# One gather of nine edge blocks as single-row fetches on SyncE, with SyncE's order written out

## The chip, the cores and the metric

The kernel runs on one core of a Trainium2 chip. The metric is device time in microseconds (us) of one execution; lower is better. A core has engines with their own instruction streams: TensorE (PE, matrix products), VectorE (DVE), ScalarE (ACT), GpSimd (POOL) and SyncE (SP). They meet through semaphores. DMA transfers are issued from the queues of SyncE, ScalarE and GpSimd and run on 16 shared DMA engines.

## What is computed

A graph layer over 8192 nodes of 256 channels and 131072 edges, sorted by destination. The part that the change touches is the message passing; the rest is attention inside groups of 32 nodes, dense layers and a layer norm:

```python
ea  = edge_attr @ w_e + b_e                       # [131072, 64] @ [64, 256]
msg = relu(x[src] + ea)                           # x[src]: a gather of rows of x
agg = segment_sum(msg, dst, num_segments=8192)
t = x + agg
h_local = bn(relu(t @ w1 + b1) @ w2 + b2 + x)
h_attn  = bn(attention(x in groups of 32, 4 heads) @ out_w.T + out_b + x)
out = h_local + h_attn
out = bn(out + relu(out @ m_w1 + m_b1) @ m_w2 + m_b2)
y = layernorm(x + out)
```

## The kernel before

Edges are worked in 128 blocks of 1024 (`BE`), two blocks (a pair) per turn of the main loop; nodes in 16 chunks of 512 (`CH`), eight blocks to a chunk.

One block passes through these steps. `gather` (L151) issues eight indirect DMAs from GpSimd; each fetches 128 rows of 1 KB, the source rows of 128 edges, into the tile `xs`, which has four buffers, so four blocks. The first 20 blocks (`NX`) gather from `x`; later ones from `xb`, a copy of `x` with the bias `b_e` added, which `copy_load` and `copy_store` (L594, L599) make in the first seven pairs. `load_edges` (L166) brings the edge attributes with four DMAs from SyncE into `ea` (two buffers). `edge_transpose` (L182, VectorE) turns them, which frees the `ea` buffer; `edge_products` (L190) multiplies them by `w_e` into PSUM; `edge_messages` (L214) adds products and gathered rows on VectorE (L223), in two halves per block, which frees the `xs` buffer, and ScalarE applies the relu (L227). `edge_hot`, `edge_sums` (L239) and `edge_place` (L259) make the segment sums with one-hot matmuls and add them to the chunk's transposed nodes `xT` (L276).

The node work is four streams of generators: `attention_front` (L409: load of the node rows `xn`, transposes, q and k), `attention_back` (L437: v, scores at L461, softmax, block-diagonal weights `bd` at L488, attention output `oT` at L496, output layer at L508), and `dense` (L517: the layers at L527, the sum with `xn` into `y` at L567, layer norm, and the store of `y` at L580). The class `Work` hands them out: `run(us)` takes steps from the streams in turn until their stated prices add up to `us`, and a stream that yields `REST` is passed over in the next calls: the count of 2 falls by one at the start of each call. A chunk's `xn` is loaded when its front begins, and a REST follows (L411, L412). `xn`, `xT` and `hA` have four buffers, `y` has one.

The order of the work: PE's order is as the program states it (`manual_schedule(engines={PE})`, L670). VectorE and ScalarE follow the stated order up to block 26 (`NV`) and after that the scheduler's; SyncE's queue has the scheduler's order throughout. In the main loop (L708 to L739) a pair issues its gathers for the next pair, then products, next edges and messages of the first block, sums of the pair before, the same of the second block, and node work in three calls, `run(0.3 * per)`, `run(0.2 * per)` and `run(0.5 * per)`, with the copies, the placing and the one-hots between. From block 104 (`TAIL`) on a planner (L741 to L786) decides by the times at which it expects each block's rows (`came`, 10.06 us per block) which step comes next. SyncE has one queue: a DMA that waits for its buffer holds up all behind it.

The functions that the change touches, as they were:

Of the kernel before, what the change touches and what calls it, by code (L numbers as in the profile page):

```python
# [8 lines left out]

FP = mybir.dt.float32  # L10
I32 = mybir.dt.int32
AF = mybir.ActivationFunctionType
ALU = mybir.AluOpType
AX = mybir.AxisListType
PSUM = bass.MemoryType.PSUM
DRAM = bass.MemoryType.DRAM
PE = mybir.EngineType.PE

P = 128
N, C, E, ED, H, NPG = 8192, 256, 131072, 64, 4, 32  # L20
# [3 lines left out]
NB = E // BE  # L24
# [20 lines left out]
RS = 1.0 / (1.0 + 1e-5) ** 0.5  # L45
LN_EPS = 1e-5
REST = -1.0


def slack(b):  # L50
# [21 lines left out]
def gnn_kernel(ctx: ExitStack, tc: tile.TileContext, x, src, dst, edge_attr, w, out):  # L72
# [31 lines left out]

    srci = const.tile([P, NB, TB], I32, name="srci")
    rel = const.tile([P, NB, TB], FP, name="rel")
    wrow = const.tile([P, NB], FP, name="wrow")
    width = const.tile([1, 1], I32, name="width")
    we = const.tile([P, C], FP, name="we")
# [36 lines left out]
        return pps.tile([P, 2, CH], FP, name="pe", tag="pe", bufs=2)  # L146


    xs_of = {}

    def gather(b):  # L151
        xs = epool.tile([P, NH, TJ, C], FP, name="xs", tag="xs", bufs=4)
        for h in range(NH):
            for j in range(TJ):
                idx = srcd[:, b * NH + h, j : j + 1] if b < ND else srci[:, b, h * TJ + j : h * TJ + j + 1]
                nc.gpsimd.indirect_dma_start(  # L156
                    out=xs[:, h, j, :],
                    out_offset=None,
                    in_=x if b < NX else xb[:, :],
                    in_offset=bass.IndirectOffsetOnAxis(ap=idx, axis=0),  # L160
                )
        xs_of[b] = xs
# [42 lines left out]
                    )  # L205
            pe_of[b, h] = pe

    def next_edges(b):
        if b < NB:
            edge_transpose(b)  # L210
        if b + 2 < NB:
            load_edges(b + 2)

    def edge_messages(b):  # L214

        xs = xs_of.pop(b)
        msg = msg_of[b] = epool.tile([P, NH, TJ, C], FP, name="msg", tag="msg", bufs=3)
        n = 2 if b < NB - 1 else 1
        for h in range(0, NH, 2):
            pe = pe_of.pop((b, h))  # L220
            for u in range(0, 2, n):
                hs = slice(h + u, h + u + n)
                nc.vector.tensor_add(  # L223
                    msg[:, hs].rearrange("p u i c -> p i u c"), pe[:, :, u : u + n, :],
                    xs[:, hs].rearrange("p u i c -> p i u c"),
                )
                nc.scalar.activation(msg[:, hs], msg[:, hs], AF.Relu)  # L227

    def edge_hot(b):
# [54 lines left out]
    with tc.tile_pool(name="setup", bufs=1) as sp:  # L284
# [122 lines left out]


    def attention_front(n0, st, pool, bank):  # L409
        if "xn" not in st:  # L410
            load_nodes(n0, st, pool)  # L411
            yield REST  # L412
        xn = st["xn"]
        xT = st["xT"] = pool.tile([P, KC, CH], FP, name="xT", tag="xT", bufs=4)
        hA = st["hA"] = pool.tile([P, KC, CH], FP, name="hA", tag="hA", bufs=4)
        for k in range(KC):
            ps = bank()
            for t in range(TN):
                nc.tensor.transpose(ps[:, t * P : (t + 1) * P], xn[:, t, k * P : (k + 1) * P], ident)
            nc.scalar.copy(xT[:, k, :], ps)  # L420
            nc.scalar.activation(
                hA[:, k, :], xT[:, k, :], AF.Identity, scale=s12[:, k : k + 1], bias=cA[:, k : k + 1]
            )
        yield 0.9

        qk = st["qk"] = pool.tile([P, 2 * KC, CH], FP, name="qk", tag="qk")
        for o in range(2 * KC):
            ps = bank()
            for k in range(KC):
                nc.tensor.matmul(  # L430
                    ps, inT[:, k, o * P : (o + 1) * P], xT[:, k, :], start=(k == 0), stop=(k == KC - 1)
                )
# [81 lines left out]
            st["done"] = o == KC - 1  # L514
            yield 1.7

    def dense(n0, st, pool, bank, t_a=0, t_z=TN, own=("h1", "m1", "zT", "y", "")):  # L517

        assert st["done"]
        nt = t_z - t_a  # L520
# [50 lines left out]
        rstd = pool.tile([P, TN], FP, name="rstd", tag="rstd" + own[4])  # L571
        nc.scalar.activation(rstd[:, :nt], mv[:, :nt, 1], AF.Sqrt, bias=eps_t)
        st["dense"] = t_z == TN
        yield 0.9 * part
        nc.vector.reciprocal(rstd[:, :nt], rstd[:, :nt])
        for t in range(nt):
            nc.vector.tensor_scalar(
                y[:, t, :], y[:, t, :], mv[:, t, 0:1], rstd[:, t : t + 1], ALU.subtract, ALU.mult
            )
        nc.sync.dma_start(out[ds(n0 + t_a * P, nt * P), :].rearrange("(t p) c -> p t c", p=P), y)  # L580
        yield 0.0


# [83 lines left out]
    PER_X = 4.2  # L667
    OTHER = ("vn", "qk", "oT", "pr", "o")
    placed = -1
    with tc.manual_schedule(engines={PE}):  # L670

        def last_of(c, t_z=TN):

# [2 lines left out]
        def summed(c, t_z=TN):  # L676
            last = last_of(c, t_z)
            return lambda: placed >= last and chunk[c].get("done") and not xp_of and b > 2

        for c in range(NCH):  # L680
            st, before, same = chunk[c], chunk[c - 1], chunk[c - 4]
            front = attention_front(c * CH, st, npool, bank)
            if c < 2:
                next(front)
            work.add(
                FRONT,
# [21 lines left out]
        while b < TAIL:  # L708
# [21 lines left out]
            copy_store(b // 2 - 1)  # L730
            copy_load(b // 2)
            if sums:
# [13 lines left out]
        while l < NB:  # L746
# [21 lines left out]
            elif t >= times[2]:  # L768
                if p + 2 < NB:
                    gather(p + 2)  # L770
                edge_products(p)
                next_edges(p + 2)
                edge_hot(p)
                t += 2.1
                p += 1
# [8 lines left out]
            else:  # L784
                t = work.step(t, min(times))
        work.finish()  # L786
    fast.close()


# [121 lines left out]
```

## Time and profile before

| | us |
|---|---|
| median of 3 runs | 2020.08 (2013.88 to 2028.74) |
| the profiled execution | 2009.84 |
| its span, first to last instruction | 2008.1 |
| PE busy | 1441.2 (72%) |
| POOL busy | 980.5 (49%) |
| VectorE, ScalarE busy | 784.8 (39%), 590.0 (29%) |
| mean granted TensorE clock | 0.82 of full speed |
| 1024 gathers (L156), each | 0.946 (median) |
| additions of messages (L223), each | 1.207 (128x1024), two of 0.657 (128x512) |
| DMAs of edge attributes (L172), issue on SyncE, each | 0.432 |

In the profile's lines a name with L is a line of the kernel; "x16" counts instructions; a wait is named after what ended it, "issue" is time in which the engine waited for nothing that the profile shows, and "remote" or "another core or an unknown queue" a release whose origin the records don't show. The ends of matmuls are modelled, and matmuls are pipelined, so a recorded matmul may still be at work. The page's throttle row gives the granted TensorE clock in tenths for 40 slices of the span.

### The profile page before, as it was taken

Reading aid. Unit: us, or ns where it says so; the run is one execution under the profiler, and the core shown is the slowest. Engines: PE = TensorE matmul, PEld = TensorE weight load, DVE = VectorE, ACT = ScalarE, POOL = GpSimd, SP = SyncE. Lnnn points to the kernel's source line nnn. Section 1 sums busy time; section 2 is a strip of 40 time slices with the busy share of each in tenths; the row PEclk is TensorE's granted clock in tenths of the full one; section 3 lists DMA queues with packets and bytes.
Section 4 is the critical chain, followed back from the end, with each engine's and each line's share of the span. In section 5 each row is a group of like instructions: output and inputs, shape, how many; then the busy total and the mean of one; then the engine's idle time right before and its main releaser. Section 6 shows DMA issues by size and latency. Waiting matters only on the chain.

```text
span 2008.1 us, 20804 instructions
## 1 busy us (share of the span) xinstructions
PE 1441.2 (72%) x7635; PEld 811.8 (40%) x7635; DVE 784.8 (39%) x1349; ACT 590.0 (29%) x840; POOL 980.5 (49%) x1032
## 2 busy tenths in 40 slices
PE   2787777786686867678587776876668687777667
PEld 1444434443343434344344333443334344343445
DVE  3444524433333333333435234351433434353434
ACT  1322322332323223232323323232232322333224
POOL 7455545454454444455364453544535354554540
PEclk7887888787787868788798887878779787897879
DMA  7586534443343434344344342443424343443430
GB/s 199 172 249 203 178 101 108 128 123 108 100 114 110 110 112 105 95 129 121 97 126 126 97 124 78 121 120 90 142 68 121 99 121 103 124 113 109 130 100 12
DMA packets 148904, 240.33 MB, mean 120 GB/s; under 512 B 27934, under 2 KB 112188, under 8 KB 148028
## 3 DMA queue, kind: packets, MB, share of 16 engines
q0 software_dynamic: 49152, 134.28, 24.2%
q1 hardware_dynamic: 98556, 104.65, 18.2%
q8 instruction: 62, 1.02, 0.2%
q14 instruction: 46, 0.38, 0.1%
q10 hardware_dynamic: 1088, 0.00, 0.0%
HBM read 222.06 MB, written 16.78 MB: 119 GB/s over the span
## 4 chain that ended last, share of the span: by engine, by line
PE 41%; another core or an unknown queue 29%; DVE 11%; issue 9%; ACT 7%; DMA 2%; DVEq 0%; SPq 0%; POOL 0%; ACTq 0%
PE at L527 12%; PE pe L203 9%; PE pw L246 6%; PE at L430 4%; DVE msg L223 4%; PE at L508 3%; PE l L267 2%; ACT msg L227 2%; PE pe L198 2%; ACT pr L471 1%; PE at L444 1%; DVE bd L488 1%; DVE eaT L185 1%; PE at L564 1%
## 5 line engine op out<-in xcount | busy, mean ns | idle before, releaser
L156 POOL DMA_INDIRECT xs<-xb,srci x864 | 818.7, 948 | 843.3 <-DVE msg L223 494.0
L227 ACT ACTIVATE msg<-msg 128x1024 f32<-128x1024 f32 (+1 forms) x258 | 269.8, 1049 | 520.8 <-DVE msg L223 430.1
L223 DVE TENSOR_TENSOR msg<-pe,xs 128x1024 f32<-128x1024 f32 (+1 forms) x258 | 304.2, 1195 | 141.2 <-remote 55.3
L203 PE MATMUL pe<-we,eaT 64*128 64x256 f32 x2048 | 308.3, 432 | 35.3 <-issue 17.9
L246 PE MATMUL pw<-msg,oh 128*32 128x256 f32 x2048 | 225.1, 451 | 108.2 <-issue 96.7
L203 PEld LDWEIGHTS pe<-we,eaT 64*128 64x128 f32 x2048 | 219.2, 213 | 157.8 <-issue 101.9
L156 POOL DMA_INDIRECT xs<-in_x_dram,srci x144 | 143.7, 998 | 121.0 <-DVE msg L223 41.9
L246 PEld LDWEIGHTS pw<-msg,oh 128*32 128x32 f32 x2048 | 83.1, 122 | 235.5 <-issue 202.3
L527 PE MATMUL at<-hA,mw 128*128 128x512 f32 (+2 forms) x304 | 135.8, 580 | 38.4 <-ACT oT L503 37.2
L185 DVE STREAM_TRANSPOSE eaT<-ea 128x512 f32<-128x512 f32 x128 | 90.2, 704 | 163.3 <-PE pe L203 88.0
L430 PE MATMUL at<-xT,inT 128*128 128x512 f32 x256 | 131.9, 643 | 8.3 <-ACT qk L433 3.6
L276 DVE TENSOR_TENSOR xT<-l,xT 128x352 f32<-128x352 f32 (+14 forms) x107 | 44.0, 433 | 227.2 <-remote 167.4
L527 PE MATMUL at<-xT,w 128*128 128x512 f32 (+2 forms) x152 | 87.9, 711 | 60.1 <-DVE xT L276 33.8
L527 PE MATMUL at<-m,mw 128*128 128x512 f32 (+2 forms) x304 | 119.7, 536 | 0.9 <-issue 0.8
L267 PE MATMUL l<-oh,ws 128*128 128x160 f32 (+4 forms) x512 | 89.0, 312 | 37.6 <-ACT ws L252 29.4
L267 PEld LDWEIGHTS l<-oh,ws 128*128 128x128 f32 x512 | 78.1, 201 | 68.9 <-ACT ws L252 37.9
L471 ACT COPY pr<-pe 32x256 f32<-32x256 f32 x128 | 46.4, 362 | 191.4 <-remote 138.2
L527 PE MATMUL at<-h,w 128*128 128x512 f32 (+2 forms) x152 | 77.4, 640 | 32.7 <-ACT h L534 23.5
L508 PE MATMUL at<-oT,outT 128*128 128x512 f32 x128 | 72.5, 695 | 35.8 <-ACT oT L503 23.1
L527 PEld LDWEIGHTS at<-hA,mw 128*128 128x128 f32 x304 | 57.8, 207 | 92.8 <-issue 48.8
L543 ACT ACTIVATE m<-at,vec 128x512 f32<-128x512 f32 (+2 forms) x76 | 46.7, 618 | 121.9 <-remote 67.7
L433 ACT ACTIVATE qk<-at,vec 128x512 f32<-128x512 f32 x64 | 43.7, 685 | 129.3 <-PE at L430 58.1
(111 smaller groups left out, 1260.2 us busy)
## 6 DMA issues: line engine op xcount, KB each, us to landing
ea<-in_edge_attr_dram SPq DMA_DIRECT2D x512, 128.0 KB
xs<-xb,srci POOLq DMA_INDIRECT x864
xn<-in_x_dram SPq DMA_DIRECT2D x16, 512.0 KB
out_dram<-y SPq DMA_DIRECT2D x14, 512.0 KB
xp<-in_x_dram SPq DMA_DIRECT2D x10, 512.0 KB
xb<-xp SPq DMA_DIRECT2D x10, 512.0 KB
xp<-in_x_dram SPq DMA_DIRECT2D x3, 1024.0 KB
xb<-xp SPq DMA_DIRECT2D x3, 1024.0 KB
```

What stands on the lines that cost most here:

```text
L156: nc.gpsimd.indirect_dma_start(out=xs[:, h, j, :], out_offset=None, in_=x if b < NX else xb[:, :], in_offset=bass.IndirectOffsetOnAxis(ap= ...
L185: nc.vector.transpose(eaT, ea[:, QR:].rearrange("p (g d) -> p g d", d=ED)[:, :, :QR])
L203: nc.tensor.matmul(pe[:, i, u, :], eaT[rows, h + u], we[rows, :], start=(b >= NX), stop=True, skip_group_check=True)
L223: nc.vector.tensor_add(msg[:, hs].rearrange("p u i c -> p i u c"), pe[:, :, u : u + n, :], xs[:, hs].rearrange("p u i c -> p i u c"),)
L227: nc.scalar.activation(msg[:, hs], msg[:, hs], AF.Relu)
L246: nc.tensor.matmul(pw[h * WN : (h + 1) * WN, i, :], oh[:, h * TJ + j, :], msg[:, h, j, :], start=(j == 0), stop=(j == TJ - 1), skip_group_ ...
L267: nc.tensor.matmul(l2[:, k, at : at + wn], ws[:, i, k * P : (k + 1) * P], oh2[:, i, :wn], start=(i == 0 and k == 0), stop=(i == last), ski ...
L430: nc.tensor.matmul(ps, inT[:, k, o * P : (o + 1) * P], xT[:, k, :], start=(k == 0), stop=(k == KC - 1))
L471: nc.scalar.copy(pr[q, :, 2 * hh : 2 * hh + 2, :].rearrange("p t s k -> p s t k"), two4[q, :, :, q])
L508: nc.tensor.matmul(ps, outT[:, k, o * P : (o + 1) * P], oT[:, k, :], start=(k == 0), stop=(k == KC - 1))
L527: nc.tensor.matmul(ps, wt[:, k, o * P : (o + 1) * P], act[:, k, :], start=(k == 0), stop=(k == nk - 1))
L543: nc.scalar.activation(m1[:, o, :], layer(mw1, KC, o, hA), AF.Relu, bias=v_("m_b1", o))
```

## The change

In nine blocks (17, 31, 44, 57, 70, 83, 96, 109, 122) the last of the eight gathers is left out. Its 128 rows are fetched one by one by SyncE into a tile `xr` (two buffers): a register load takes 16 byte offsets at a time from `srcs`, a clamped and scaled copy of the source indices, and each row is a DMA of 1 KB. The main loop issues 20 rows per pair at five points, the tail 10 per block. The second half of such a block's messages is three additions in place of one.

SyncE's queue now keeps the stated order too. The loads of edges are put off by one or two points in the pair (`catch_up`, about half a pair), the store of a chunk's `y` by four points (two pairs), and the node rows of chunk c+4 are loaded two points after chunk c's sum with `xn`, ahead of the front that uses them; the front still rests. The third call of node work, `run(0.5 * per)`, is split in 0.3 and 0.2.

In the built orders GpSimd has 1015 gathers instead of 1024; SyncE has 1152 row DMAs and 72 register loads more; the matmuls are the same ones in a partly different order.

```diff
+ROW = 4 * C
+RT = NH * TJ - 1
+ROW_BLOCKS = (17, *range(31, NB, 13))
+RB, RL = 10, 16
...
+    def row_stream():
+        for b in ROW_BLOCKS:
+            while len(xr_of) > 1 or not (b < NX or copied[0]):
+                yield 0
+            xr = xr_of[b] = epool.tile([P, C], FP, name="xr", tag="xr", bufs=2)
+            for e0 in range(0, P, RL):
+                _, rows = nc.values_load_multi_w_load_instructions(
+                    srcs[b : b + 1, e0 : e0 + RL], engines=[SP], min_val=0, max_val=(N - 1) * ROW,
...
+                for i, row in enumerate(rows):
+                    p = (e0 + i) % EQ * QR + (e0 + i) // EQ
+                    nc.sync.dma_start(xr[p : p + 1, :].bitcast(U8), flat[b >= NX][ds(row, ROW)].unsqueeze(0))
+                    if e0 + i == P - 1:
+                        xr_full.add(b)
+                    yield 1
...
+    def fetch_rows(n):
+        for _ in range(n):
+            next(row_by_row, None)
...
     def gather(b):
...
+                if b in ROW_BLOCKS and h * TJ + j == RT:
+                    continue
...
+    def put_off(turns, do):
+        later.append([turns, do])
+
+    def catch_up(n=1):
+        for entry in list(later):
+            entry[0] -= n
+            if entry[0] <= 0:
+                later.remove(entry)
+                entry[1]()
+
-    def next_edges(b):
+    def next_edges(b, turns=0):
...
+            if turns:
+                put_off(turns, lambda: load_edges(b + 2))
+            else:
+                load_edges(b + 2)
...
     def edge_messages(b):
...
+                if b in ROW_BLOCKS and h + u + n == NH:
...
+                    nc.vector.tensor_add(msg[:, hs, 0, :], pe[:, 0, u : u + n, :], xs[:, hs, 0, :])
+                    for v in range(u, u + n - 1):
+                        nc.vector.tensor_add(msg[:, h + v, 1, :], pe[:, 1, v, :], xs[:, h + v, 1, :])
+                    nc.vector.tensor_add(msg[:, NH - 1, 1, :], pe[:, 1, u + n - 1, :], xr)
...
+        nc.vector.tensor_scalar(srcs, srci_r[:, RT * P : (RT + 1) * P], 0.0, float(N - 1), ALU.max, ALU.min)
+        nc.vector.tensor_scalar(srcs, srcs, float(ROW), None, ALU.mult)
...
-        if "xn" not in st:
-            load_nodes(n0, st, pool)
+        if "rested" not in st:
+            if "xn" not in st:
+                load_nodes(n0, st, pool)
             yield REST
...
+        catch_up(1000)
         y = pool.tile([P, nt, C], FP, name="y", tag=own[3])
...
+            put_off(2, load_ahead)
...
+        if turns:
+            put_off(turns, store)
+        else:
+            store()
...
-    with tc.manual_schedule(engines={PE}):
+    with tc.manual_schedule(engines={PE, SP}):
...
-                work.add(DENSE, summed(c), dense(c * CH, st, npool, bank))
+                work.add(DENSE, summed(c), dense(c * CH, st, npool, bank, turns=4))
...
-                next_edges(b + 2)
+                next_edges(b + 2, 1)
                 edge_messages(b)
+            fetch_rows(2 * RB // 5)
...
-            next_edges(b + 3)
+            next_edges(b + 3, 2 if b else 1)
             edge_messages(b + 1)
+            fetch_rows(2 * RB // 5)
             work.run(0.3 * per)
+            catch_up()
+            fetch_rows(2 * RB // 5)
...
             work.run(0.2 * per)
+            catch_up()
+            fetch_rows(2 * RB // 5)
             for i in blocks:
                 edge_hot(i)
-            work.run(0.5 * per)
+            work.run(0.3 * per)
+            fetch_rows(2 * RB // 5)
+            work.run(0.2 * per)
...
                 edge_products(p)
+                catch_up()
                 next_edges(p + 2)
+                fetch_rows(RB)
```

More of the change, by code (lines that the diff above doesn't have):

```diff
@@ L11 @@
 I32 = mybir.dt.int32
+U8 = mybir.dt.uint8
 AF = mybir.ActivationFunctionType
@@ L17 @@
 PE = mybir.EngineType.PE
+SP = mybir.EngineType.SP
+ACT = mybir.EngineType.Activation
 P = 128
@@ L106, in gnn_kernel @@
     rel = const.tile([P, NB, TB], FP, name="rel")
+    srcs = const.tile([P, P], I32, name="srcs")
     wrow = const.tile([P, NB], FP, name="wrow")
@@ L146, in bank2 @@
         return pps.tile([P, 2, CH], FP, name="pe", tag="pe", bufs=2)
-    xs_of = {}
+    xs_of, xr_of, xr_full = {}, {}, set()
+    flat = [a.bitcast(U8).rearrange("n c -> (n c)") for a in (x, xb[:, :])]
+    copied = [False]
+    def row_stream():
[6 more added lines that the diff above has]
+                    srcs[b : b + 1, e0 : e0 + RL], engines=[SP], min_val=0, max_val=(N - 1) * ROW,
+                    skip_runtime_bounds_check_because="the indices are clamped to the rows of x when they are kept",
+                )
+                for i, row in enumerate(rows):
[4 more added lines that the diff above has]
+                    yield 1
+    row_by_row = row_stream()
+    def fetch_rows(n):
+        for _ in range(n):
+            next(row_by_row, None)
     def gather(b):
@@ L206, in edge_products @@
             pe_of[b, h] = pe
-    def next_edges(b):
+    later = []
+    def put_off(turns, do):
[7 more added lines that the diff above has]
+    def next_edges(b, turns=0):
         if b < NB:
@@ L515, in attention_back, with dense @@
             yield 1.7
-    def dense(n0, st, pool, bank, t_a=0, t_z=TN, own=("h1", "m1", "zT", "y", "")):
+    def dense(n0, st, pool, bank, t_a=0, t_z=TN, own=("h1", "m1", "zT", "y", ""), turns=0):
         assert st["done"]
@@ L573, in dense, with load_ahead @@
         st["dense"] = t_z == TN
+        if turns and n0 // CH + 4 < NCH:
+            c = n0 // CH + 4
+            def load_ahead():
+                if "xn" not in chunk[c]:
+                    load_nodes(c * CH, chunk[c], pool)
+            put_off(2, load_ahead)
         yield 0.9 * part
@@ L579, in dense, with store @@
             )
-        nc.sync.dma_start(out[ds(n0 + t_a * P, nt * P), :].rearrange("(t p) c -> p t c", p=P), y)
+        def store():
+            nc.sync.dma_start(out[ds(n0 + t_a * P, nt * P), :].rearrange("(t p) c -> p t c", p=P), y)
+        if turns:
+            put_off(turns, store)
+        else:
+            store()
         yield 0.0
```

14 lines of the change are left out of this document (9 added, 5 removed).

## The prediction

> **What bounds the kernel now.** I read the page's busy table first, then the waits of GpSimd, then the chain that ended last, then the timeline of one stretch in which the chain names no engine, and last the waits of SyncE's queue.
>
> The busy table and the throttle row show no engine that is full:
>
> ```profile
> PE 1441.2 (72%) x7635; PEld 811.8 (40%) x7635; DVE 784.8 (39%) x1349; ACT 590.0 (29%) x840; POOL 980.5 (49%) x1032
> ...
> PEclk7887888787787868788798887878779787897879
> ```
>
> POOL, which issues the 1024 gathers, is busy for half of the span. One gather takes 0.946 us and 0.30 us pass before the next, so a run of them goes at 1.25 us each. The rest of POOL's time is waiting for the messages that free an `xs` buffer:
>
> ```profile
> POOL xs L156 <- DVE msg L223: 535.9, 51, 21.2
> POOL xs L156 <- issue: 292.0, 946, 2.8
> POOL xs L156 <- DVE oh L256: 141.0, 18, 16.2
> ```
>
> So POOL works in bursts: between 250 and 1650 us the trace has 45 bursts of 16 gathers (two blocks), each 19.7 us long, with a pause of 11.2 us on average behind it. 23 of the 44 pauses last 5.8 to 8.5 us, the other 21 last 11.4 to 21.2 us. That is what the kernel's time is made of in this stretch: bursts and pauses. What keeps the messages late? The chain gives a share that it can put on no engine:
>
> ```profile
> PE 41%; another core or an unknown queue 29%; DVE 11%; issue 9%; ACT 7%; DMA 2%; DVEq 0%; SPq 0%; POOL 0%; ACTq 0%
> ```
>
> The timeline of the burst at 507 us shows what this is. (Columns: start, duration, engine, line, operation; in brackets the idle time before and what ended it.)
>
> ```profile
> 507.16 0.94 POOL L156 DMA_INDIRECT xs<-xb,srci  x1 [18.97 <-DVE msg L223]
> ...
> 511.33 1.35 PE L267 MATMUL l<-oh,ws 128*128 128x160 f32 x8
> ...
> 521.44 0.69 ACT L503 ACTIVATE oT<-at,vec 128x512 f32<-128x512 f32 x1 [6.92 <-remote]
> ...
> 525.92 0.95 POOL L156 DMA_INDIRECT xs<-xb,srci  x1 [0.31 <-issue]
> ...
> 529.95 0.62 DVE L276 TENSOR_TENSOR xT<-l,xT 128x448 f32<-128x448 f32 x1 [18.59 <-remote]
> ...
> 540.06 1.23 DVE L223 TENSOR_TENSOR msg<-pe,xs 128x1024 f32<-128x1024 f32 x1 [4.84 <-PE pe L203]
> ...
> 543.28 0.95 POOL L156 DMA_INDIRECT xs<-xb,srci  x1 [16.41 <-DVE msg L223]
> ```
>
> The matmuls of L267 are recorded at 511.3, but VectorE, which waits for nothing but their result, goes on at 529.95, 3.1 us after the last gather of the burst ended (525.92 + 0.95). The records of PE run ahead of its work. PE is behind for most of the burst, catches up after it, then come the messages, and they start the next burst. In the table of windows PE is busy 5.06 of 14.37 us in 512.5 to 526.9 (share 0.35) and 12.64 of 16.41 us in 526.9 to 543.3 (share 0.77). Over the 45 bursts the late ends of PE's work lie 1.6 or 3.1 us behind the end of the burst again and again. Why PE is slow while gathers run, the trace does not say; that it is, it does.
>
> SyncE's queue is not in this:
>
> ```profile
> SPq L172 <- DVE eaT L185: 1118.8, 76, 33.2
> SPq L282 <- DVE st L569: 149.9, 8, 25.5
> SPq L580 <- DVE y L577: 136.7, 11, 42.4
> ```
>
> It waits for free `ea` buffers for more than half of the span, and the transposes of L185 waited for an edge load once, 1.4 us in all.
>
> **The change, part by part.** The sum is made on the profiled execution: 2009.84 us, its span 2008.1. That is 0.5% under the median of 2020.08, so the result is scaled by 1.0051 at the end.
>
> *Nine gathers leave POOL.* 9 x 1.25 = 11.3 us of bursts. If the next burst starts that much earlier each time, all of it is gained; if PE only needs its work done, less. In the cycles with short pauses (half of them) the pause holds little but the landing and the messages: full 1.25 us. In those with long pauses PE gets 0.35 x 1.25 = 0.44 us less done inside the burst and makes it up at 0.77: 0.57 us, leaving 0.68. The mean is 0.97, times 9: **-8.7 us**. Bounds -11.3 and 0 (a burst that is shorter without PE being done sooner).
>
> *Messages of these nine blocks.* One addition of 128x1024 (1.20 us) becomes one of 128x512 (0.66, the two of the last block) and two of 128x256 (nearest: the half-size addition of L567, 0.425): 1.51, so +0.31 x 9 = 2.8 us, on the path where the freed buffer starts the next burst. Four or five of the nine are second blocks of a pair, whose buffers the burst reaches 8 gathers later. **+1.4**; bounds 0 and 2.8.
>
> *1152 row fetches and 72 register loads on SyncE.* Price of a row, from its smallest and its costliest DMA: 0.231 (1 KB for `vec`) and 0.568 us (64 rows for `we`); a register load is 0.50 (the one of `width`). 20 rows per pair of blocks are 4.6 to 11.4 us, loads 0.6, the eight edge loads 8 x 0.43 = 3.5: 9 to 16 us per pair, and the shortest cycle has 26.1. In the tail 10 rows per block are 5.2 to 7.8 us with its edge loads, and a block there takes 15. The cover is the 1118.8 us in which SyncE waits for `ea` buffers. By the built order a block's rows are all issued well before its messages (block 31: in the pair before), so no message waits for them. **0**; where the cover goes, see the rivals. The bytes are those of the gathers they replace.
>
> *Edge loads, stores, node rows.* In the stated order SyncE still stops at each edge load until its buffer is free, so a load is late only by what is put in front of it: up to 16 rows, 3.7 to 9 us. It is needed a pair later (26 us or more). Stores two pairs later: `y` is written again four pairs later, and a forced catch-up stands before it. Node rows ahead: nobody waited for them (PE waited 0.2 us before L419, for an edge load). Queued behind a waiting node load or store are edge loads and rows; that wait (149.9 and 136.7 us) exists today and hides in the same slack. **0**; at best the 1.4 us of the one late edge load.
>
> *Two VectorE operations at the start* (128x128 on `srcs`): at most 0.41 us each by L577's 128x256. They stand before the copies of `srci`, behind which the first gathers from `x` wait, but PE transposes meanwhile. **+0.4**; bounds 0 and 0.8.
>
> *PE's order.* `work.run` is now called four times per pair, and a REST lasts two calls, so attention resumes sooner. I counted matmuls of the built orders at full-clock prices (0.43 us for 512 columns and pass) between the last score matmul and the first `oT` matmul of a chunk: mostly 11 to 20 us before, 9 to 17 after, but 1.6 in the second chunk and 5.4 in a late one (the least before was 4.5, and PE did not wait there). The softmax between them took 11.1 us in the second chunk and 14 to 32 us in later ones, where VectorE was itself held by PE. If PE waits, edge products are queued behind. High: 11.1 - 1.6 = 9.5, and 22.5 - 7.0 (5.4 at share 0.77) = 15.5, together 25. Low: 0, since a late chain is mostly late through PE; a gain is not excluded either, see below. I take **+4**, nearest to the low end, because the case with 4.5 cost nothing.
>
> Sum: -8.7 + 1.4 + 0.4 + 4 = -2.9; 2009.84 - 2.9 = 2006.9; times 1.0051: **2017 us**. Ends: -11.3 gives 2009, +28.6 gives 2049.
>
> **The rivals.** Less than 1% either way (2000 to 2040) is about what a measurement of this kernel can't tell from no change.
>
> *The shorter burst gives nothing* (same; 0.10). PE's work is unchanged, and if its lateness is its own, the burst only happens to end with it. For: PE's share 0.77 even behind the bursts. Against: the ends at 1.6 and 3.1 us behind the burst. 2017 + 8.7 = 2026 us. Beside it: the Trainium skill (SBUF — State Buffer, section on the two separate sides) says that DMA and engine accesses use separate ports and can't slow each other; by that rule this rival holds. The trace, 0.35 against 0.77, speaks for some contention, though not for which.
>
> *PE waits for the softmax* (slower; 0.22). Place: L496 behind L488. It decides when the softmax takes longer than the cover, in the two chunks above all: +25 instead of +4, and the full 2.8 for messages: 2009.84 - 8.7 + 28.6 = 2029.7, scaled 2040. A wait that pushes a message past the end of a burst also turns a short pause into a long one, 7 us into 14 for one of them: 2047 us.
>
> *SyncE becomes the bound* (slower; 0.05). It decides when a row costs more than (26.1 - 4.1)/20 = 1.1 us. At 1.5 us a pair takes 34 us where the mean cycle is 30.9: 58 pairs x 3.1 = 180, about 2190. Against: SyncE issues one DMA after the other every 0.23 to 0.57 us, while the first landing comes 2.1 us (median of 512 edge loads) after the issue, so it does not wait for each. Beside it: the Trainium skill (DMA: Bandwidth & Descriptors, rules for kernel authors and the anatomy of one DMA) gives a fixed 2 us per DMA and advises against many small ones; if the rows went one at a time, 20 x 2 + 4 = 44 us per pair, some 2700 us, an estimate by that page.
>
> *The new order shortens pauses* (faster; 0.18). 21 pauses are long because attention or dense steps stand in front of the edge products. The finer calls move these steps; if three of 21 fall from 16 to 7 us, 27 us go: 1990. The same lottery can lose as much.
>
> **How the numbers follow.** The forecast has 0.45, with the first rival 0.55 near 2017 to 2026, of which 0.02 reaches below 2000 and 0.02 above 2040. Faster 0.18 + 0.02 = 0.20; same 0.51; slower 0.22 + 0.05 + 0.02 = 0.29. The range reaches from the faster rival, 1990, to just above the softmax rival, 2050; outside are SyncE as the bound and the far parts of both, 0.2.
>
> **What would show it.** Right: 1015 gathers; nine bursts of 18.5 us; the same late PE behind bursts; SyncE still waiting hundreds of microseconds for `eaT`; no wait of VectorE for `xr`. Wrong: L496 waiting for `bd` by more than 10 us; `eaT` waiting for edge loads; rows above 1 us each; a mean pause other than 11 us by more than 1, which 45 times over is more than all else here.

## The result, and the profile after

The changed kernel takes 2074.73 us (median of 4 runs, 2063.42 to 2079.32), the kernel before 2017.86 in the same runs: ratio 1.0265, 95% interval 1.0206 to 1.0323. It is 57 us slower. The forecast was 2017, with a range from 1990 to 2050.

One thing has to be known for the numbers that follow: the kernel before took 2018 to 2019 us beside this result and in one group of the experiments, and 1324 us in the other four groups, though runs of both kinds came from a chip of the same number. So each kernel is compared only with the kernel before in its own group of runs; I write "the 2018 setting" and "the 1324 setting".

The profiled execution of the changed kernel has a span of 2072.2 us, 64.1 more than before. The busy table:

```profile
PE 1415.5 (68%) x7635; PEld 819.6 (40%) x7635; DVE 782.9 (38%) x1369; ACT 590.5 (28%) x838; POOL 969.9 (47%) x1023
...
PEclk7777787878688888878778797878888788798779
```

The engines are busy for about as long as before (TensorE 1415.5 us against 1441.2) and the granted clock is nearly the same (0.811 against 0.822); the 64 us are waiting. The waits of GpSimd:

```profile
POOL xs L191 <- DVE msg L281: 508.3, 50, 32.0
POOL xs L191 <- issue: 287.3, 933, 2.8
POOL xs L191 <- DVE oh L314: 193.0, 17, 22.9
POOL xs L191 <- DVE msg L278: 46.0, 4, 18.6
```

The bursts of gathers together are 14 us shorter (1256.5 us against 1270.7; nine gathers of 1.25 us are 11.3 of it), and the pauses between them 86 us longer (763.9 against 677.7). By the start of block 26's gathers 44 us are lost, by block 30's 54; after that the distance stays between 46 and 76. So most of the loss is there after the first quarter of the blocks. In the chain that ended last the share of DMA goes from 2% to 4%:

```profile
PE 44%; another core or an unknown queue 23%; DVE 11%; issue 11%; ACT 4%; DMA 4%; SPq 1%; POOL 1%; DVEq 0%; ACTq 0%
```

The waits of TensorE name a load behind this. (Columns: engine, line, what ended the wait; us in all, times, longest.) L480 is the old L419, the transposes of a chunk's node rows `xn`:

```profile
PE at L480 <- DMA xn<-in_x_dram: 72.7, 9, 18.0
PE pe L522 <- issue: 59.1, 47, 8.7
...
PE at L557 <- DVE bd L549: 14.8, 4, 6.0
PE pe L238 <- DVE eaT L220: 13.1, 6, 4.1
```

Before, the profile has no wait of TensorE for `xn` at all. Now there are nine. The time from the issue of a node load to the first transpose was 18.6 us before (median of the last twelve chunks) and is 4.9 now, which is hardly more than such a load takes to land (by the semaphore updates in the traces, a median of 4.3 us after and 4.1 before: the loads are not slower, they go out later). The other view is SyncE's queue:

```profile
SPq L207 <- DVE eaT L220: 493.8, 64, 32.8
SPq L680 <- DVE xp L679: 51.8, 7, 26.6
SPq L652 <- DVE y L647: 41.0, 3, 28.4
```

Of the 1118.8 us in which SyncE waited for free `ea` buffers, 493.8 are left: the rows take up the rest. The longest of the nine waits, in the timeline:

```profile
1757.43 0.76 PE L325 MATMUL l<-oh,ws 128*128 128x144 f32 x4
...
1761.80 1.76 SPq L207 DMA_DIRECT2D ea<-in_edge_attr_dram  x4
...
1763.66 6.21 SPq L173 DMA_DIRECT2D xr<-xb  x10
...
1769.97 0.42 SPq L340 DMA_DIRECT2D xn<-in_x_dram  x1
...
1776.16 1.97 PE L480 MATMUL at<-ident,xn 128*128 128x128 f32 x8 [17.97 <-DMA xn<-in_x_dram]
```

TensorE is done at 1758.2 and needs the node rows. SyncE stands at an edge load whose buffer is not free until 1761.8 (3.6 us of TensorE's wait), issues its four DMAs (1.8), then ten rows (6.3), and only then the node load, which lands 6.2 us later. That is the change in one picture: an urgent load behind a load that waits and behind rows that are in no hurry.

### The profile page after: what moved, and what is told of

Same layout as the page of the kernel before. It is cut to its first block, busy times and chain, and to the rows that moved or that the text cites. A ratio compares the mean times of both kernels' runs of the same rounds, so it can differ in the third digit from the quotient of the medians.

```text
span 2072.2 us, 23022 instructions
## 1 busy us (share of the span) xinstructions
PE 1415.5 (68%) x7635; PEld 819.6 (40%) x7635; DVE 782.9 (38%) x1369; ACT 590.5 (28%) x838; POOL 969.9 (47%) x1023
## 4 chain that ended last, share of the span: by engine, by line
PE 44%; another core or an unknown queue 23%; DVE 11%; issue 11%; ACT 4%; DMA 4%; SPq 1%; POOL 1%; DVEq 0%; ACTq 0%
PE at L588 14%; PE pe L238 10%; PE pw L304 5%; DVE msg L281 4%; PE at L491 4%; PE at L569 2%; PE l L325 2%; PE at L505 2%; DMA xn<-in_x_dram 1%; DMA ea<-in_edge_attr_dram 1%; ACT msg L285 1%; PE pe L233 1%; PE pe L522 1%; PE at L480 1%
## 5 line engine op out<-in xcount | busy, mean ns | idle before, releaser
L238 PE MATMUL pe<-we,eaT 64*128 64x256 f32 x2048 | 307.9, 440 | 55.1 <-DVE msg L281 20.9
L281 DVE TENSOR_TENSOR msg<-pe,xs 128x1024 f32<-128x1024 f32 (+1 forms) x249 | 292.9, 1201 | 118.9 <-ACT m L604 27.6
L588 PE MATMUL at<-hA,mw 128*128 128x512 f32 (+2 forms) x304 | 152.0, 632 | 89.6 <-ACT qk L494 40.4
L304 PE MATMUL pw<-msg,oh 128*32 128x256 f32 x2048 | 167.6, 420 | 43.3 <-issue 42.1
L588 PE MATMUL at<-m,mw 128*128 128x512 f32 (+2 forms) x304 | 128.8, 566 | 14.3 <-issue 9.3
L304 PEld LDWEIGHTS pw<-msg,oh 128*32 128x32 f32 x2048 | 73.7, 118 | 128.8 <-issue 100.6
L588 PE MATMUL at<-xT,w 128*128 128x512 f32 (+2 forms) x152 | 80.6, 674 | 42.6 <-DVE xT L334 22.9
L588 PE MATMUL at<-h,w 128*128 128x512 f32 (+2 forms) x152 | 85.5, 686 | 26.9 <-issue 10.5
L522 PE MATMUL pe<-qk 64*128 64x128 f32 x512 | 54.7, 324 | 71.8 <-issue 59.1
L480 PE MATMUL at<-ident,xn 128*128 128x128 f32 x128 | 29.9, 387 | 107.0 <-DMA xn<-in_x_dram 72.7
```

Source lines behind the costliest of these rows:

```text
L238: nc.tensor.matmul(pe[:, i, u, :], eaT[rows, h + u], we[rows, :], start=(b >= NX), stop=True, skip_group_check=True)
L281: nc.vector.tensor_add(msg[:, hs].rearrange("p u i c -> p i u c"), pe[:, :, u : u + n, :], xs[:, hs].rearrange("p u i c -> p i u c"),)
L304: nc.tensor.matmul(pw[h * WN : (h + 1) * WN, i, :], oh[:, h * TJ + j, :], msg[:, h, j, :], start=(j == 0), stop=(j == TJ - 1), skip_group_ ...
L522: nc.tensor.matmul(two[:, s, a : a + P], qk[s * DH : (s + 1) * DH, hh, a : a + P], qk[s * DH : (s + 1) * DH, KC + hh, a : a + P], start=Tr ...
L588: nc.tensor.matmul(ps, wt[:, k, o * P : (o + 1) * P], act[:, k, :], start=(k == 0), stop=(k == nk - 1))
```

## The experiments

The first theory after the result (A) was that the order of TensorE costs, since the calls of node work are finer; the rivals, that SyncE's stated order costs by itself (B), or the rows do (C). Four kernels take them apart: an empty row list; the last two calls joined; both; and the kernel before with the split alone. They and the four after them ran in the 1324 setting; where a forecast names times near 2018 only, it has to be read as a loss against the kernel before.

**split**, in the kernel before:

```diff
-            work.run(0.5 * per)
+            work.run(0.3 * per)
+            work.run(0.2 * per)
```

> The kernel before with one edit, the last call of a pair (0.5) split into 0.3 and 0.2: the order of TensorE is that of the changed kernel, matmul for matmul, and nothing else of the change is there (SyncE's order is left to the scheduler, no rows). If the order of TensorE costs, 2060 to 2080 us, with the loss before block 30; if SyncE's stated order or the rows cost, 2005 to 2030.

Measured: 1325.28 us against 1323.86, ratio 1.0010 (1.0000 to 1.0020). Theory A falls for this setting: the same matmuls in the same order as in the changed kernel (both traces list the same 7635 in one order) cost 1 us.

**onerun_norows**, in the changed kernel:

```diff
-ROW_BLOCKS = (17, *range(31, NB, 13))
+ROW_BLOCKS = ()
...
-            work.run(0.3 * per)
             fetch_rows(2 * RB // 5)
-            work.run(0.2 * per)
+            work.run(0.5 * per)
```

> Both undone: the calls joined and no row fetched. TensorE, ScalarE and GpSimd have the order of before, VectorE too but for two small operations at the start; only SyncE's order and the places of its loads and stores are changed. If SyncE's stated order costs by itself, 2060 to 2080 us; if the order of TensorE or the rows cost, 2013 to 2029, as before.

Measured: 1332.02, ratio 1.0061 (1.0044 to 1.0078). SyncE's stated order with its moved loads costs 8 us. B has a small part.

**norows**, the first edit of these alone:

> The changed kernel with an empty list of row blocks: all 1024 rows of blocks are gathered by GpSimd again; the finer calls, the later edge loads and stores, the node rows ahead and SyncE's stated order stay. If the order of TensorE (the finer calls) is what costs, 2065 to 2080 us, and the pauses of the first 30 blocks are as long as in the changed kernel. If SyncE's stated order costs, also 2065 to 2080. If the row fetches cost (SyncE busy with them in front of edge loads and node rows), 2020 to 2030.

Measured: 1342.30, ratio 1.0144 (1.0126 to 1.0163). Neither forecast: 18 us, more than B alone. TensorE waits for node rows in two chunks:

```profile
PE at L480 <- DMA xn<-in_x_dram: 20.1, 2, 14.9
```

With the finer calls the rest between load and transposes is two of four calls of a pair instead of two of three, and the load cannot be issued early any more, because SyncE follows the stated order: in split these two chunks' node rows went out 26 and 82 us before their transposes, here 10 and 15. Two edits that cost 1 and 8 us alone cost 18 together.

**onerun**, the second edit alone:

> The changed kernel with the last two calls of the work list in a pair joined into one again (0.5 of the pair). The built order of TensorE is then that of the kernel before, matmul for matmul; rows, edge loads, stores, node rows and SyncE's stated order stay changed. If the order of TensorE costs, 2005 to 2020 us, with the first 30 blocks within 10 us of before. If SyncE's stated order or the rows cost, 2060 to 2080.

Measured: 1361.52, ratio 1.0283 (1.0257 to 1.0309). Against onerun_norows the rows cost 29.5 us (and 11 more, since nine gathers went). Theory C holds the most.

The next four ask by what way.

**after_again**, the changed kernel unchanged:

> The changed kernel itself, on the chip of the runs of this call, beside the kernel before. On a chip on which the kernel before takes 1324 us: the finer calls with SyncE's stated order cost 18 us without rows, the rows cost 29.5 us with the old order; if the two add, 1324 + 8 + 10 + 29.5 = 1372 us; if both only make the same node rows late, about 1360. On a chip on which the kernel before takes 2018 us, 2063 to 2080 as before.

Measured: 1408.05 against 1324.30, ratio 1.0630 (1.0604 to 1.0656). More than the sum: with the finer calls the rows cost 66 us instead of 29.5.

```profile
PE at L480 <- DMA xn<-in_x_dram: 80.4, 10, 19.5
```

In this setting the idle time of TensorE accounts for nearly all of it: span less busy time is 131 us in split and 206 in after_again, 76 more, and the spans differ by 80.3 (1324.9 and 1405.2); the idle time before L480 grew by 79. The node loads themselves land a little later in this setting (5.7 us against 4.5 in split, medians). The starts of the gathers tell where it arises: against split, norows has lost its 15 us by block 24 and loses no more, and after_again has lost 23 by then, 58 by block 126 and 80 at the end.

**midrows**, `ROW_BLOCKS = tuple(range(44, 100, 13))`:

> The changed kernel with rows for five blocks only (44, 57, 70, 83, 96): none is fetched for the first 30 blocks' use and none in the last 24. If the rows cost where they stand in front of node rows and of the last edge loads, this gives the time of the changed kernel without rows less 5 x 1.25 = 6 us (1336 us where the kernel before takes 1324). If each row costs everywhere, half of the rows' price stays: 5/9 of 29.5 = 16 us more than without rows, 1358 us.

Measured: 1375.21, ratio 1.0380 (1.0362 to 1.0398): 33 us over norows for five blocks, 51.1 us of waits at L480. Each row costs where it stands, in the steady part too, and more than the second forecast said.

**freeSP**, `manual_schedule(engines={PE})` again:

> The changed kernel with SyncE's order left to the scheduler again, as in the kernel before; rows, finer calls and later loads stay. If the stated order costs (node rows late behind waits), within 10 us of the kernel before; if SyncE's time for the rows costs, nothing is gained against the changed kernel.

Measured: 1397.02, ratio 1.0551 (1.0533 to 1.0568), 74.1 us at L480. Without the stated order 11 us come back, no more: the scheduler too puts rows in front of node loads (16 in front of one of them in this trace).

**xnahead**, node loads of the third and fourth chunk a pair earlier:

```diff
+            if b in (2, 4):
+                load_nodes((b // 2 + 1) * CH, chunk[b // 2 + 1], npool)
             if b:
```

> The changed kernel with one edit: the node rows of the third and fourth chunk are loaded at the head of the second and third pair, before that pair's edge loads, instead of half a pair before their transposes. If TensorE's wait for these rows is the price of SyncE's stated order, 10 to 20 us less than the changed kernel on the same chip, and no wait of L480's matmuls for node rows of over 5 us is left before block 30. If the rows take SyncE's time from the edge loads all along, less than 8 us of difference.

Measured: 1401.54, ratio 1.0576 (1.0557 to 1.0595). The waits at L480 fall from 80.4 to 54.1 us, those of the two chunks are gone, and 6.5 us are gained. This is under the 8 us of the second forecast. So a microsecond less of this wait is not a microsecond less of time; what took its place is not shown.

The following four ran in the 2018 setting.

**rows_alone**, freeSP and the joined calls together, so TensorE's order is that of before and SyncE's is left to the scheduler as before:

> The changed kernel with the last two calls of a pair joined (TensorE's order of the kernel before) and SyncE's order left to the scheduler: of the change the row fetches and the nine gathers less remain, with the later edge loads and stores as far as the scheduler keeps them. If node rows late behind rows cost, the waits before L480 are 25 to 35 us as in the kernel with the calls joined (31.3), and the time is 1.5 to 3% over the kernel before. If SyncE's stated order was the cause there, it is within 0.7% of the kernel before.

Measured: 2088.35 against 2018.98, ratio 1.0343 (1.0268 to 1.0419). The rows, with the moved loads and stores and without nine gathers, cost 69 us, about as much as the whole change. Both forecasts are missed: more time than either, and only 20.9 us of waits at L480. TensorE also waits for transposed edges at its edge products; VectorE waited only 3.0 us for edge loads, so why the transposes are late is not shown.

```profile
PE pe L238 <- DVE eaT L220: 31.7, 11, 5.9
...
PE at L480 <- DMA xn<-in_x_dram: 20.9, 3, 12.3
```

**xnact**, node loads from the third chunk on by ScalarE's DMA queue:

```diff
-        nc.sync.dma_start(xn, x[ds(n0, CH), :].rearrange("(t p) c -> p t c", p=P))
+        q = nc.sync if isinstance(n0, int) and n0 < 2 * CH or not isinstance(n0, int) else nc.scalar
+        q.dma_start(xn, x[ds(n0, CH), :].rearrange("(t p) c -> p t c", p=P))
```

> The changed kernel with one edit: from the third chunk on, the node rows (L340) are asked for on ScalarE's DMA queue instead of SyncE's, at the same place of the program; TensorE's order is that of the changed kernel. If TensorE's waits for node rows that stand behind rows and edge loads in SyncE's queue are what costs (80.4 us before L480 in 1408 us, 75.0 in 2074 us), these waits fall below 20 us and the time by 50 to 70 us against the changed kernel: 1340 to 1360 us where the kernel before takes 1324, 2005 to 2025 where it takes 2018. If late edge loads or late rows cost, it stays within 20 us of the changed kernel.

Measured: 2139.60 against 2018.98, ratio 1.0602 (1.0524 to 1.0679). A miss. The waits at the transposes are gone (5.2 us), and the kernel is slower. SyncE and TensorE have new waits:

```profile
SPq L207 <- DMA xn<-in_x_dram: 100.6, 4, 30.3
SPq L173 <- DMA xn<-in_x_dram: 93.6, 4, 24.7
```

```profile
PE pe L238 <- DVE eaT L220: 129.0, 49, 11.0
```

The node load on the other queue takes one of the same eight DMA semaphores in turn (the one issued at 513.65 us and SyncE's next edge load at 518.06 both use number 104), so SyncE's queue stops until ScalarE has issued the load and it has landed: 194 us in eight stops. The edit replaced a wait by another one; it does not test what it was made for.

**rest4**, `self.rest[i] = 4` in place of 2:

> The changed kernel with a rest of four calls of the work list (a whole pair) instead of two between the load of a chunk's node rows and their transposes; SyncE's stated order, the rows and all loads stay. The order of TensorE changes with it. If node rows come late because they are asked for half a pair before their use, the load goes out 15 us or more before the transposes instead of 4 to 8, the waits before L480 fall below 25 us, and the time falls by 40 to 70 us against the changed kernel. If SyncE's time for the rows costs by the edge loads, less than 15 us are gained.

Measured: 2160.41 against 2018.98, ratio 1.0716 (1.0629 to 1.0803). A miss: a loss of 141 us where less than the 57 of the changed kernel was forecast. No wait at L480 is left, and TensorE waits 95.6 us for the transposed edges instead, though VectorE waited for edge loads by only 1.6 us; so late edge loads are not the reason. The order of TensorE has changed with the rest, so this run cannot say how much of that the rows cause. It does say that, in this order, node rows in time are not enough.

**nogather**, in the kernel before the nine gathers left out, nothing in their place:

> The kernel before with the last of the eight gathers left out in the nine row blocks and nothing fetched in its place: the last 128 edges of such a block take the source rows of the group before (part of the computation is changed), in the three additions of the changed kernel. It prices the first two terms of the sum by themselves. Forecast: 9 gathers and the messages together -7.3 us, between -11.3 and +2.8; on a chip on which gathers follow each other without a pause, -11 us.

Measured: 1999.92 against 2018.98, ratio 0.9889 (0.9820 to 0.9959): 8 to 36 us gained. The profiled execution is one that shows no gain (span 2009.3 us): bursts shorter by 11.6 us, pauses longer by 15.

```profile
POOL xs L160 <- DVE msg L233: 515.2, 48, 23.7
POOL xs L160 <- issue: 289.4, 938, 2.7
POOL xs L160 <- DVE oh L266: 139.8, 17, 17.3
POOL xs L160 <- DVE msg L231: 37.0, 4, 14.7
```

Still open was by what the rows cost: by SyncE's time, or by the buffers and additions around them. One group of runs, in the 1324 setting:

**norows_b**, the kernel of norows:

> The changed kernel with no row block, once more, on the chip of the runs of this call: the finer calls, the stated order, the later loads and stores, 1024 gathers. Where the kernel before takes 1324 us, 1342 as before. Where it takes 2018: if the rows are the cost, 2010 to 2035; if finer calls and stated order carry it there, 2060 to 2080.

Measured: 1345.97 against 1324.48, ratio 1.0163 (1.0145 to 1.0180).

**onedma**, in the changed kernel:

```diff
-            for e0 in range(0, P, RL):
...
+            nc.sync.dma_start(xr, (x if b < NX else xb)[b * NPB : b * NPB + P, :])
+            xr_full.add(b)
+            yield 1
```

> The changed kernel, but each row block's buffer is filled by one DMA of 128 neighbouring rows of the same source (part of the computation is changed: the last 128 edges of nine blocks take other source rows). Nine gathers less, the three additions, the buffers, the finer calls and the stated order stay; 9 DMAs instead of 1152 and no register loads. If SyncE's time for single rows in front of node and edge loads is the cost, the time is that of the kernel without rows or up to 12 us less. If the additions, the buffers or the scheduler's order cost, it stays within 15 us of the changed kernel (1408 where the kernel before takes 1324, 2075 where it takes 2018).

Measured: 1334.70, ratio 1.0064 (1.0041 to 1.0087). All of the change is there but 1143 of the 1152 DMAs and the register loads, and of the changed kernel's loss of 84 us (after_again, another group of the same setting) 10 are left. It is 11.3 us under norows_b, as nine gathers of 1.25 us would make it; the intervals leave some 4 us either way. SyncE's wait for free `ea` buffers is back, and the waits at the transposes (here L472) are those of norows:

```profile
SPq L199 <- DVE eaT L212: 675.1, 101, 19.2
```

```profile
PE at L472 <- DMA xn<-in_x_dram: 20.0, 2, 15.5
```

**twice**, each row fetched twice:

```diff
-                    nc.sync.dma_start(xr[p : p + 1, :].bitcast(U8), flat[b >= NX][ds(row, ROW)].unsqueeze(0))
+                    for _ in range(2):
+                        nc.sync.dma_start(xr[p : p + 1, :].bitcast(U8), flat[b >= NX][ds(row, ROW)].unsqueeze(0))
```

> The changed kernel with each row fetched twice into the same place: 2304 DMAs and the same result. If SyncE's time for the rows is the cost, the loss against the kernel without rows doubles or more: over 1460 us where the kernel before takes 1324, over 2120 where it takes 2018, with SyncE's waits for free edge buffers near nothing. If something else of the change costs, within 15 us of the changed kernel.

Measured: 2700.47, ratio 2.0379 (2.0313 to 2.0445). More than a doubled dose: the second fetch has the same target as the first and waits until that has landed, 1.2 us each time.

```profile
SPq L174 <- DMA xr<-xb: 1212.5, 1024, 4.8
SPq L174 <- DMA xr<-in_x_dram: 178.6, 128, 7.5
...
SPq L208 <- DVE eaT L221: 13.0, 4, 7.3
```

```profile
PE at L481 <- DMA xn<-in_x_dram: 666.8, 14, 69.3
PE pe L239 <- DVE eaT L221: 469.3, 55, 22.8
```

Here SyncE is the bound: it waits for no edge buffer any more, and node rows and edges are both late.

A last group, in the 1324 setting again, repeats two of these and adds rest4.

**norows_c:**

> The changed kernel with no row block, 1024 gathers. Where the kernel before takes 1324 us: 1342 to 1346, as in two calls before. Where it takes 2018: the rows cost there by themselves 69 us, so 2010 to 2035 is expected; 2060 to 2080 would mean that the stated order and the finer calls carry a loss of their own there.

Measured: 1346.58 against 1324.85, ratio 1.0176 (1.0151 to 1.0201).

**onedma_c:**

> The changed kernel with one DMA per row block (part of the computation is changed: the last 128 edges of nine blocks take other source rows). Where the kernel before takes 1324 us, 1335 as before. Where it takes 2018: if SyncE's time for single rows is the cost there too, 1995 to 2030, below the kernel without rows by 5 to 20 us; if the loss there has another cause, 2055 to 2080.

Measured: 1333.89, ratio 1.0069 (1.0045 to 1.0093), 12.7 us under norows_c.

**rest4_b:**

> The changed kernel with a rest of four calls between the load of node rows and their transposes. Where the kernel before takes 2018 us, 2160 as before. Where it takes 1324: the waits before L480 go from 80 us to under 10 there too; if they are the only way by which the rows cost, 1335 to 1350 us; if edge loads are late next, as where the kernel before takes 2018 (eaT 148 us), over 1380.

Measured: 1428.30, ratio 1.0764 (1.0724 to 1.0803). The waits at L480 go from 80.4 to 4.9 us, and this replaces them:

```profile
PE pe L238 <- DVE eaT L220: 102.8, 57, 7.3
```

As in the 2018 setting, the time comes back at the edge products; here VectorE waited for edge loads by 27.6 us, so late edge loads are a part of it at most. My theory that the late node rows are the only way by which the rows cost is not borne out; whether the new wait is the rows' doing or that of the changed order was not tried (rest of four without rows).

No version of these beats the kernel before; only nogather does, and it leaves work out.

## Why the prediction was wrong

*What failed: "1152 row fetches and 72 register loads on SyncE ... 0".* rows_alone shows +69 us in the 2018 setting, with the gain of nine gathers and the moved loads in it, and onedma shows in the 1324 setting that it is SyncE's single DMAs: 74 of 84 us go with them. Three parts of the step were wrong.

First, the cover. I took the 1118.8 us that SyncE waits for `ea` buffers as room for the rows. For the edge loads that was right: from the issue of a block's last edge DMA to its transpose it is 27.5 us before and 28.3 after (medians), and VectorE waited for an edge load by 8.6 us in all. But the queue carries other loads, and the room that counts is that of the tightest: node rows, with 18.6 us before and 4.9 after.

Second, "Node rows ahead: nobody waited for them". True before, and the price 0 did not follow. The load was not ahead in the queue: it went out half a pair before its use, and the stated order put in front of it an edge load that waits for its buffer and rows, ten of them in the wait shown above. I had written that "queued behind a waiting node load or store are edge loads and rows", and did not ask what a node load is queued behind.

Third, the price of a row. My bound was 0.231 to 0.568 us, from the durations of other DMAs, and 0.50 for a register load. From one row's issue to the next it is 0.74 us on average, register loads included: 0.49 between gathers and 1.00 while gathers run; a register load takes 1.2 us (median of 72). 1152 rows are 852 us, 41% of the span. This was outside the bounds, by a cause that the rows of before did not show: its edge loads take 0.42 us to issue during bursts and 0.41 between them (see the last section). But the price did not decide: in the 1324 setting a row takes 0.52 us, inside the bound, and the loss is larger, 84 us. Part of it is waiting that I had put at nothing: edge loads and rows take eight semaphores in turn, so a row waits until the DMA eight places before it has landed, 34 us in all in the 2018 setting and 127 in the other, there mostly for edge loads.

*What held.* The nine gathers: the bursts are 14 us shorter where 11.3 were forecast, and their worth is -8.7 forecast, -11.3 and -12.7 measured by onedma against norows in the 1324 setting, -8 to -36 by nogather in the 2018 setting. The messages (+1.4) are inside these numbers and cannot be told from them. The start: the second burst began 1.1 us later, forecast 0.4. TensorE's order, +4 with ends 0 and 25: in the 1324 setting 1 us by split; in the 2018 setting the waits of L557 for `bd` are 14.8 us against 2.7, inside the ends, though over the 10 us that were to be a sign of being wrong. (In the row fetches' sum, the tail's lower end of 5.2 us comes to 4.4 by its own terms; nothing hangs on it.)

*The rivals.* "SyncE becomes the bound" was the right place with the wrong condition: it was to decide above 1.1 us per row, and the loss came at 0.74, while SyncE still waited 493.8 us for buffers. A queue need not be full to be late; it is late for the load that has least time. Only twice is the case as I had described it. "The shorter burst gives nothing" is not what the runs show on average, though the one profile of nogather looks like it. "PE waits for the softmax" has 15 us of waits for it, not 25 of loss; in split the same wait is 25.0 us with the time 1 us longer, so there it stands in place of other waits. The pauses did get longer and not shorter; the finer calls by themselves gave neither gain nor loss in split, which ran in the 1324 setting only.

*What stays open.* In the 2018 setting the changed kernel without rows was not run, so what stated order and finer calls cost there is not known; by the intervals of rows_alone and the whole change it is some 11 us at most, if the moved loads that rows_alone keeps cost nothing there. That the single DMAs are the cause is shown in the 1324 setting, by onedma; that the same holds in the 2018 setting is argued from rows_alone. How much of the loss goes by node rows and how much by edge products is not settled either: xnahead, xnact and rest4 removed waits at the node rows, and the time fell by less or rose.

## What to carry to other kernels

Before work is put on a queue that seems to have time, list what the queue carries and take the load with the least time between its issue and its use, not the queue's waits in sum. Writing out a queue's order takes away the scheduler's freedom to issue a load early, so every load behind a waiting one inherits its wait (here 11 of 84 us came back with that freedom). And a wait that is removed by an edit is only worth its length if nothing else is late behind it: look up what the engine waits for next.

## What the runs showed of the hardware

The two settings differ in something that none of the busy columns names. In split, the kernel before but for its finer calls, GpSimd waits for messages by 2.7 us in all and TensorE is busy for 90% of the span; the gathers themselves take the same 0.95 us:

```profile
PE 1194.2 (90%) x7635; PEld 726.2 (55%) x7635; DVE 779.2 (59%) x1349; ACT 588.1 (44%) x838; POOL 986.8 (74%) x1032
...
PEclk8998999999999999998998988989899999999999
```

The rows make it visible, because each stands behind a register move, an instruction of SyncE that transfers nothing. (Columns: minimum, median and maximum in ns.) The changed kernel in the 2018 setting, and the same kernel in the 1324 setting:

```profile
L173 SPq MOVE xr<-xb x1024: 2/29/1410, 338.4 to 1972.7; - x171
L173 SPq DMA_DIRECT2D xr<-xb x1024: 2/228/1410, 338.5 to 1973.3; - x171
```

```profile
L173 SPq MOVE xr<-xb x1024: 29/29/29, 238.9 to 1320.3; - x171
L173 SPq DMA_DIRECT2D xr<-xb x1024: 227/228/309, 239.0 to 1321.5; - x171
```

In the 1324 setting a move takes 0.029 us. In the 2018 setting nearly one in four takes over 0.3 us while gathers run, mostly 0.70, and one in 20 between bursts, all of these within 3 us of a burst's last gather. So what is slow during gathers is not only TensorE, as the prediction had it: some of SyncE's instructions are too, in steps of 0.70 us. What makes these steps, and what sets the setting, the traces do not show. The granted clock is lower there (0.82 against 0.96), but a factor of 1.17 does not give the 1.52 between the two times.

The Trainium skill (SBUF — State Buffer, section on the two separate sides) says that transfers and engine accesses use separate ports and can't slow each other. The 1324 setting agrees: gathers run nearly without a pause and TensorE is at 90%. The slowness of the 2018 setting alone does not speak against that rule, since it holds up SyncE's register moves as well, which transfer nothing; no run here separates the two. The Trainium skill (DMA: Bandwidth & Descriptors, section on the anatomy of one DMA) puts the fixed cost of a DMA from GpSimd's queue at about 2 us, most of it the wait for the landing. The prediction used that figure for SyncE's queue. In twice, where SyncE waits for each 1 KB row to land, it is 1.4 us (0.23 of issue and 1.2 of waiting); no run here shows it for GpSimd's. That twice takes the 2700 us which the prediction estimated with that figure is chance: it issues two DMAs for each row and waits for the first.
